# SyncE's transfers in the order of the program, and the last exchange's first round behind the residual's load

## The chip, the core and the metric

The kernel runs on one core of a Trainium2 chip. TensorE multiplies, VectorE, ScalarE and GpSimd work on the results, and SyncE only issues transfers (DMAs). Each engine runs its own list of instructions strictly in the order in which they stand there, and waits for the others by semaphores. The metric is the device time of one execution in microseconds.

## The reference

Attention with a conditioning vector, over 8 batches of 512 rows, 512 features and 16 heads of 32, and the input is added at the end:

```python
Q = _split_heads(x @ Wq.T + bq)
K = _split_heads(x @ Wk.T + bk)
V = _split_heads(x @ Wv.T + bv)
tQ = _split_heads(tokens @ Wq.T + bq)
tK = _split_heads(tokens @ Wk.T + bk)
cQ = Q + tQ
cK = K + tK
scores = jnp.einsum('bhqd,bhkd->bhqk', cQ, cK) / jnp.sqrt(jnp.float32(HEAD_DIM))
attn = jax.nn.softmax(scores, axis=-1)
out = jnp.einsum('bhqk,bhkd->bhqd', attn, V)
...
x = x + attention
```

## The kernel before

**Tiles and stages.** Work is cut into 32 tiles, numbered 0 to 31: tile t is batch t // 4 and a group of four heads. A loop calls `thirds(t)` for the tiles 1 to 28; one call is a stage. What stands ahead of the loop (loads, tile 0, the beginning of tile 1) and behind it (tiles 29 to 31) is written out by hand. A stage finishes tile t-1 (`weighted`: the product of its softmax weights with V, L839, then its sums, its output), computes row maxima and part of the weights of tile t+1, the rest of the weights of tile t, and three pieces of the projections of a later batch. The stage's parts i = 0, 1, 2 are the three thirds. A stage begins, on TensorE, with the L839 matmuls of `weighted`.

**Two halves of the weights.** For the first 256 query rows of a tile the weights that were made for the row maxima are kept (`kept`, in `store`); for the other 256 they are computed again in the transposed form that the product needs. `weighted` takes the fresh half first and the kept half second. The kept half has to be transposed. VectorE turns its 32x32 blocks in four pieces (`turn_kept`, L659: two pieces in the first third of the stage before its own, one at the end of each other third), and the blocks are then exchanged between groups of 32 partitions by transfers.

**The exchange.** `swap_kept(t, move)` has three rounds of six transfers (L681): move 0 puts a block aside, move 1 copies its partner into its place, move 2 brings the one put aside to the partner's place. Each transfer waits for the landing of the one ahead of it in its chain of three. In an ordinary tile SyncE issues two of move 0 and all of move 1 (eight), GpSimd four of move 0 and all of move 2; in every fourth tile SyncE issues all of move 0 too (twelve). For the last kept tile, 29, SyncE issues move 0 and half of each of the others. Moves 0 and 1 of tile t+1 stand at the end of stage t, move 2 in the middle third of stage t+1, ahead of `split_max` (GpSimd, L714 to L717) and `turn_max` of the following tile.

**SyncE's other transfers.** In each stage: `send` writes the output of tile t-1 (L916, four transfers, after GpSimd's last addition, L913); `load_blocks` loads four pieces of x for a later batch (L172, until x is used up in stage 22), which VectorE turns (L371); `turn_max` transposes the maxima (maxT, L726, after GpSimd's L717), which TensorE needs at L771; `load_residual` loads x again for the last addition (xr, L190, four pieces), to which GpSimd adds the bias (`bias_residual`, L203). Tile 30's residual goes into `store`. A transfer also waits for the one eight places ahead of it on its queue.

**What sets the order.** The order of TensorE, ScalarE, VectorE and GpSimd is that of the program, because the call `manual_schedule` names these four. SyncE isn't named: a scheduler of the framework places its transfers by its own estimate of when each becomes ready, so that a load whose buffer is free may be put ahead of, or among, transfers that the program writes earlier.

Of the kernel before, what the change touches and what calls it, by code (L numbers as in the profile page):

```python
# [17 lines left out]
def kernel(  # L18
# [52 lines left out]
    KEPT = range(1, T - 2)  # L71
# [59 lines left out]
    def begin(*ws):  # L131
        for w in ws:
            rows = order[w : w + 4]
            pairs = [(j, j + 1) for j in rows if j + 1 in rows]
            last = max(
                pairs, key=lambda p: rows.index(p[0]) + rows.index(p[1]), default=sorted(rows[2:])
            )
            order[w : w + 4] = [j for j in rows if j not in last] + list(last)
        row_of[0] = list(order)

    def released(*roles):
        order[:] = [row_of[0][i] for i in roles]
# [19 lines left out]
    def spread(a, d):  # L162

        return a.rearrange("(f j) d -> j f d", j=BL)[:, :, d : d + BL]
# [12 lines left out]
    def turned_by_vector(t):  # L177

        return t < T - 1

    def load_residual(t):

        b, g = divmod(t, G)
        if turned_by_vector(t):
            if t == T - 2:
                xr[t] = late[0][:, 2, :].rearrange("p (f e) -> p f e", e=BL)
            else:
                xr[t] = op.tile([P, NB, BL], F32, tag="xr", name=f"xr_{t}")
            for h in range(HG):
                nc.sync.dma_start(  # L190
                    xr[t][h * BL : (h + 1) * BL], spread(x[b], g * P + h * BL)
                )
        else:

            xr[t] = xT[b][:, g, :]
# [31 lines left out]
    def load_w(n, w, queue, cs=range(NC)):  # L227
        wv = w.rearrange("(c p) d -> p c d", p=P)
        for c in cs:
# [7 lines left out]
                mybir.EngineType.Activation,  # L237
                mybir.EngineType.DVE,
                mybir.EngineType.Pool,
            }  # L240
        )
    )
# [353 lines left out]
    def row_max(t, qc, hold=False, w=HG, scores=True):  # L596

        if t >= T:
            return
        open_max(t)  # L600
        for j in range(HG if scores else 0):
            row_scores(t, qc, j, banks(w + j))
        if row_of[0] or t < T - 2 or t * NS + qc == T * NS - 1:
            for j in range(2) if scores else (1, 0):
                one_max(t, qc, j, banks(w + j))
        else:
            row_max_of(t, qc, 0, banks(w, 2))
        last, both = [banks(w + 2), banks(w + 3)], banks(w + 2, 2)
        apart = row_of[0] and row_of[0][w + 3] - row_of[0][w + 2] > 1

        def held():
            if apart or hold and t < T - 2:
                for j in range(2):
                    one_max(t, qc, 2 + j, last[j])
            else:
                row_max_of(t, qc, 1, both)

        if hold:
            return held
        held()  # L620
        return nothing
# [4 lines left out]
    def row_max_aside(t, qc):  # L626

        open_max(t)
        for j in range(HG):
            row_scores(t, qc, j, banks(j))  # L630
        nc.scalar.copy(spare, banks(0).rearrange("p (c f) -> p c f", f=P))  # L631
        for j in (1, 2, 3):
            one_max(t, qc, j, banks(j))

    def max_aside(t, qc):
        nc.vector.tensor_reduce(nmax[t][:, qc, 0:1, 0], spare, AX.XY, ALU.max, negate=True)
# [27 lines left out]
    def swap_kept(t, move, some=range(6)):  # L664

        later = 6 if t % 4 == 1 else 2

        def part(a, g):
            return kept[t][a * BL : (a + 1) * BL, g].rearrange("p c h s -> p (c h s)")

        for n in some:
            a, g = APART[n]
            at = (n + 2) % HG * BL
            aside = (store[:, 6:8] if t == KEPT[-1] else between)[at : at + BL, n // HG]
            aside = aside.rearrange("p i s -> p (i s)")
            to, of = [(aside, part(a, g)), (part(a, g), part(g, a)), (part(g, a), aside)][move]
            if t < KEPT[-1]:
                here = move == 2 or move == 0 and n >= later
            else:
                here = move > 0 and n >= 3  # L680
            (nc.gpsimd if here else nc.sync).dma_start(to, of)  # L681

    def denominators(t, qc, w=HG, js=range(HG)):

        if t >= T - 2:
            return
        keep = t in KEPT and qc < KQ
        if keep and t not in kept:
            kept[t] = room(t)
        for j in js:  # L690
            of = to = banks((w or 0) + j)
            if w is None and j == 0:
                of = to = spare
            if keep:
                to = kept[t][:, :, qc, j, :].rearrange("p g (c e) -> p g c e", e=BL)
                if w is None and j == 0:
                    of = spare.rearrange("p c (g e) -> p g c e", e=BL)
                else:
                    of = of.rearrange("p (c g e) -> p g c e", g=HG, e=BL)
            nc.scalar.activation(  # L700
                to,
                of,
                AF.Exp,
                bias=nmax[t][:, qc, j, :],
                accum_out=sums[t][:, qc, j, :],
            )
# [437 lines left out]
    def turn_more(t, i, after):  # L1144

        for _ in range((TURNED if t + 1 < KEPT[-1] else TURNED_LAST).get((i, after), 0)):
            if t + 1 in KEPT:
                n = turned[t + 1] = turned.get(t + 1, -1) + 1
                turn_kept(t + 1, n)
        even = t % 2 == 0  # L1150
        if (i, after) == ((2, 1) if even else (0, 2)) or (t, i, after) == (2, 0, 2):
            turn_x(next_x[0])
            next_x[0] += 1

    def thirds(t, made):

        b, r = divmod(t, G)
        of = (t - 1) // G + 1
        begin(0, HG)
        turn_more(t, 0, 0)  # L1160
        row_max_aside(t + 1, 1)
        max_aside(t + 1, 1)
        row_max(t + 1, 2, False, HG)
        turn_more(t, 0, 1)
        denominators(t + 1, 1, None, (1, 2, 3, 0))
        denominators(t + 1, 2, HG)
        weighted(t - 1, banks(0), banks(1), nothing)
        turn_more(t, 0, 2)
        load_blocks(1)
        one_item(of, *next(made), (2, 3), ignore, nothing)  # L1170
        released(0, 1, 4, 5, 7, 6, 2, 3)
        for i in (1, 2):
            begin(HG)
            rows = (t + 1, 3) if i == 1 else (t + 2, 0)
            if i == 1:
                joined(t, i - 1, rows)
                turn_more(t, i, 0)
                row_max(*rows, False, HG, False)
            else:
                exponentials_of_rest(t, i - 1)  # L1180
                turn_more(t, i, 0)
                row_max(*rows, False, HG)
            turn_more(t, i, 1)
            if i == 1:
                first = range(6 if t + 1 < KEPT[-1] else 3)
                swap_kept(t, 2, first)
                split_max(t + 1)
                turn_max(t + 1)
                swap_kept(t, 2, range(len(first), 6))
            dens = lambda js=range(HG): denominators(*rows, HG, js)  # L1190
            n, u, kind = next(made)
            if kind == "first":
                products(of, n, u, kind, False, dens, nothing, None)
                turn_more(t, i, 2)
            elif n == "v":
                small = nothing
                if t + 1 not in KEPT:
                    small = lambda: transpose_max(t + 1, banks(2), nc.scalar.copy)
                other_shared(of, n, u, dens, (0, 3), small, lambda: turn_more(t, i, 2))
                released(1, 2, 4, 5, 6, 7, 0, 3)  # L1200
            else:
                products(of, n, u, kind, False, dens, nothing, False)
                turn_more(t, i, 2)
            if i == 1:
                aparts[t] = masked(t)
            if (t + 1, i) == (KEPT[-1], 1):
                swap_kept(t + 1, 0)
            if i == 2:
                if r == 0:
                    combine_x(b + 1, 1, nc.gpsimd)  # L1210
                load_residual(t + 1)
            else:
                if t > 1:
                    bias_residual(t)
                if r == 0:
                    combine_x(b + 1, 0, nc.gpsimd)
            if i == 2 and t + 1 < KEPT[-1]:
                for move in range(2):
                    swap_kept(t + 1, move)
# [105 lines left out]
    t = T - 3  # L1325
# [46 lines left out]
    t = T - 2  # L1372
# [25 lines left out]
    t = T - 1  # L1398
# [101 lines left out]
```

## Time and profile before

| what | value |
|---|---|
| median of 3 runs | 649.41 us (649.39 to 649.48) |
| the profiled execution | 650.74 us |
| its span, first to last instruction | 648.9 us |
| granted TensorE clock | 1.000 |
| TensorE matmuls busy | 642.6 us (99%) |
| TensorE weight loads busy | 358.5 us (55%) |
| VectorE, ScalarE, GpSimd busy | 600.7 us (93%), 533.6 us (82%), 409.6 us (63%) |
| SyncE's queue of transfers, share of the 16 DMA engines | 53.3% |
| GpSimd's queue of transfers | 19.2% |

The times are from the start of the profiled span. A row of the view in order of time reads: start, duration, engine, line, operation, what is written from what is read, how many; in square brackets stands the idle time of the engine ahead of it and what ended it. Consecutive equal instructions are one row. SPq is SyncE issuing transfers: its duration is the time of issue (with the waits between the transfers of one row), not of the transfer, which lands later. In the section of the page on transfers the last number is the median time from issue to landing. "issue" as a releaser means that the view shows no other engine that ended the wait.

### The profile page before, as it was taken

To read this page: it belongs to the slowest core of one execution; us is meant where nothing else is said; L and a number is where in the kernel's file an instruction comes from. 1 tells how busy PE (TensorE), PEld (TensorE's weight loads), DVE (VectorE), ACT (ScalarE), POOL (GpSimd) and SP (SyncE) were. 2 spreads that over 40 slices of the span, in tenths; PEclk is the share of its full clock that TensorE was granted. 3 is DMA by queue.
4 is the path that set the end of the run, shared out by engine and by line. 5 is a ranking of instruction groups with operands and counts; after the bars stand their busy time and mean duration, and the time that the engine had idled before them with its cause. 6 is when DMAs were issued, how large, how long until landed. Compare 5 with 4: busy or idle time off the path is not lost. (4 is left out here: it accounts for less than half of the span.)

```text
span 648.9 us, 24878 instructions
## 1 busy us (share of the span) xinstructions
PE 642.6 (99%) x9856; PEld 358.5 (55%) x9856; DVE 600.7 (93%) x845; ACT 533.6 (82%) x1364; POOL 409.6 (63%) x651
## 2 busy tenths in 40 slices
PE   9999999999999999999999999999999999999997
PEld 8445555556555555555555555555655555555541
DVE  3799999999999999999999999999999999999887
ACT  2479888889888889888888988898988888888564
POOL 3642555767666785668566585766767677675650
PEclk9999999999999999999999999999999999999999
DMA  7634588788779788878788887897877777777821
GB/s 187 106 48 68 121 183 175 158 180 178 155 172 181 156 190 181 190 155 172 173 184 172 171 170 152 177 198 158 180 152 180 176 162 153 165 177 161 201 37 33
DMA packets 248456, 102.01 MB, mean 157 GB/s; under 512 B 229962, under 2 KB 230474, under 8 KB 248340
## 3 DMA queue, kind: packets, MB, share of 16 engines
q1 hardware_dynamic: 234196, 65.54, 53.3%
q0 software_dynamic: 12384, 33.83, 19.2%
q8 instruction: 78, 1.28, 0.8%
q10 hardware_dynamic: 1760, 1.05, 0.6%
q14 instruction: 38, 0.31, 0.2%
HBM read 19.75 MB, written 8.39 MB: 43 GB/s over the span
## 5 line engine op out<-in xcount | busy, mean ns | idle before, releaser
L592 DVE TENSOR_REDUCE nmax<-psum 128x1 f32<-128x512 f32 x279 | 177.8, 676 | 9.9 <-PE psum L640 5.1
L681 POOL DMA_DIRECT2D store<-store x258 | 128.9, 502 | 77.3 <-DMA store<-store 51.9
L700 ACT ACTIVATE psum<-psum,nmax 128x512 f32<-128x512 f32 x248 | 165.1, 678 | 3.6 <-DVE nmax L592 3.0
L640 PE MATMUL psum<-kT,qT 32*128 32x512 f32 x1024 | 161.8, 612 | 0.0
L700 ACT ACTIVATE store<-psum,nmax 128x512 f32<-128x512 f32 x204 | 139.5, 700 | 24.7 <-DVE nmax L592 24.5
L798 ACT ACTIVATE store<-psum 128x512 f32<-128x512 f32 x232 | 119.8, 603 | 33.4 <-PE psum L784 33.4
L659 DVE STREAM_TRANSPOSE store<-store 128x1024 f32<-128x1024 f32 x116 | 138.9, 1217 | 0.0
L649 DVE TENSOR_REDUCE nmax<-psum 128x2 f32<-128x1024 f32 x98 | 118.9, 1213 | 0.0
L839 PE MATMUL psum<-store,v 128*32 128x256 f32 x1856 | 107.1, 381 | 0.6 <-issue 0.6
L839 PEld LDWEIGHTS psum<-store,v 128*32 128x32 f32 x1856 | 57.2, 110 | 57.9 <-ACT wT_q L631 21.2
L784 PE MATMUL psum<-qT,kT 32*128 32x256 f32 x928 | 83.8, 373 | 0.0
L640 PEld LDWEIGHTS psum<-kT,qT 32*128 32x128 f32 x1024 | 61.3, 183 | 35.5 <-issue 17.8
L912 POOL TENSOR_TENSOR res<-res,recs 128x512 f32<-128x512 f32 x30 | 31.4, 1045 | 75.4 <-DVE res L911 75.4
L784 PEld LDWEIGHTS psum<-qT,kT 32*128 32x128 f32 x928 | 60.8, 184 | 5.7 <-issue 0.3
L700 ACT ACTIVATION_READ_ACCUMULATOR psum<-psum,nmax 128x1 f32 x248 | 55.1, 222 | 0.0
L461 PE MATMUL psum<-wc_v,xc 128*32 128x256 f32 x768 | 47.7, 379 | 0.0
L203 POOL TENSOR_TENSOR xr<-xr,bvs 128x512 f32<-128x512 f32 x30 | 38.3, 1276 | 11.1 <-DMA x<-in_x_dram 11.1
L461 PE MATMUL psum<-xc,wc_q 128*32 128x256 f32 x720 | 44.8, 379 | 0.0
L461 PE MATMUL psum<-xc,wc_k 128*32 128x256 f32 x720 | 44.5, 379 | 0.0
L700 ACT ACTIVATION_READ_ACCUMULATOR store<-psum,nmax 128x1 f32 x204 | 44.4, 218 | 0.0
L913 POOL TENSOR_TENSOR res<-res,xr 128x512 f32<-128x512 f32 x30 | 38.3, 1276 | 2.4
L461 PE MATMUL psum<-xT,wT_k 128*32 128x256 f32 x480 | 34.5, 382 | 0.0
(191 smaller groups left out, 975.4 us busy)
## 6 DMA issues: line engine op xcount, KB each, us to landing
store<-store SPq DMA_DIRECT2D x264, 128.0 KB, 2.9
store<-store POOLq DMA_DIRECT2D x258, 128.0 KB, 3.8
out_dram<-res SPq DMA_DIRECT2D x122, 64.0 KB, 3.7
xr<-in_x_dram SPq DMA_DIRECT2D x120, 64.0 KB, 3.4
x<-in_x_dram SPq DMA_DIRECT2D x112, 64.0 KB, 3.5
w_q<-in_L_cond_Wq_dram SPq DMA_DIRECT2D x4, 256.0 KB, 4.5
w_v<-in_L_cond_Wv_dram SPq DMA_DIRECT2D x16, 64.0 KB, 2.5
w_k<-in_L_cond_Wk_dram SPq DMA_DIRECT2D x16, 48.0 KB, 2.8
```

What stands on the lines that cost most here:

```text
L203: nc.gpsimd.tensor_tensor(xr[t], xr[t], bias, ALU.add)
L461: nc.tensor.matmul(pt[r], still[:, r], moving, start=(kc == kcs[0]), stop=(kc == kcs[-1]))
L592: nc.vector.tensor_reduce(nmax[t][:, qc, j : j + 1, 0], pt, AX.X, ALU.max, negate=True)
L640: nc.tensor.matmul(pt, qkT["q", t][r, qc * P : (qc + 1) * P], qkT["k", t][r, :], start=True, stop=True,)
L649: nc.vector.tensor_reduce(nmax[t][:, qc, pr * 2 : pr * 2 + 2, 0], pt, AX.X, ALU.max, negate=True)
L659: nc.vector.transpose(e, e)
L681: (nc.gpsimd if here else nc.sync).dma_start(to, of)
L700: nc.scalar.activation(to, of, AF.Exp, bias=nmax[t][:, qc, j, :], accum_out=sums[t][:, qc, j, :],)
L784: nc.tensor.matmul(banks(j)[:, i * HS : (i + 1) * HS], qkT["k", t][r, kc * P : (kc + 1) * P], qkT["q", t][r, KQ * P :], start=False, stop= ...
L798: nc.scalar.activation(e[:, j], banks(j), AF.Exp)
L839: nc.tensor.matmul(pt[j * HD : (j + 1) * HD, half * HS : (half + 1) * HS], vs[b % 2][:, kc, (g * HG + j) * HD : (g * HG + j + 1) * HD], e, ...
L913: nc.gpsimd.tensor_tensor(y, y, xr.pop(t), ALU.add)
```

## The change

SyncE is named in the call as well, so that its transfers stand in the order in which the program's text issues them. And in stage 28 the residual of tile 29 is loaded in the middle third, ahead of move 0 of tile 29's exchange, and no longer in the last third.

```diff
                 mybir.EngineType.DVE,
                 mybir.EngineType.Pool,
+                mybir.EngineType.SP,
             }
...
             if (t + 1, i) == (KEPT[-1], 1):
+                load_residual(t + 1)
                 swap_kept(t + 1, 0)
             if i == 2:
                 if r == 0:
                     combine_x(b + 1, 1, nc.gpsimd)
-                load_residual(t + 1)
+                if t + 1 < KEPT[-1]:
+                    load_residual(t + 1)
```

The lists of TensorE, VectorE, ScalarE and GpSimd are the same, row by row; the lines of the new file are one to three higher. SyncE's list has the same transfers in another order. In the rows that follow, the number behind xr, maxT and res is the tile; behind x it counts blocks of x (four to a batch); store is the exchange. A row gives the line, the operation, written from read, the shape and how many.

SyncE in stages 21 and 22, before: the exchange of tiles 21 (twelve) and 22 (two and six).

```order
L726 DMA_TRANSPOSE maxT_21_6002<-split_145 128x4x128
L190 DMA xr_21_6114<-in_x_dram 32x16x32
L172 DMA x_30_6204<-in_x_dram 32x16x32 x3
L681 DMA store_77<-store_77 32x1024 x12
L916 DMA out_0_dram<-res_20_6193 32x16x32 x4
L172 DMA x_30_6204<-in_x_dram 32x16x32
L726 DMA_TRANSPOSE maxT_22_6277<-split_145 128x4x128
L190 DMA xr_22_6380<-in_x_dram 32x16x32 x4
L172 DMA x_31_6469<-in_x_dram 32x16x32 x2
L681 DMA store_77<-store_77 32x1024 x2
L172 DMA x_31_6469<-in_x_dram 32x16x32
L681 DMA store_77<-store_77 32x1024 x6
```

The same place in the changed kernel:

```order
L727 DMA_TRANSPOSE maxT_21_6002<-split_145 128x4x128
L190 DMA xr_21_6114<-in_x_dram 32x16x32 x4
L682 DMA store_77<-store_77 32x1024 x12
L917 DMA out_0_dram<-res_20_6193 32x16x32 x4
L172 DMA x_30_6204<-in_x_dram 32x16x32 x4
L727 DMA_TRANSPOSE maxT_22_6277<-split_145 128x4x128
L190 DMA xr_22_6380<-in_x_dram 32x16x32 x4
L682 DMA store_77<-store_77 32x1024 x8
```

The loads of x no longer stand ahead of or within an exchange; all four stand behind the output and ahead of maxT. The load of xr stands whole between maxT and the exchange; before, some of it stood ahead of maxT in three of four stages.

SyncE at the start, before (tiles 0 and 1, and the blocks of batch 1 and 2, which wait for VectorE from x_6 on):

```order
L172 DMA x_5_246<-in_x_dram 32x16x32 x4
L190 DMA xr_0_553<-in_x_dram 32x16x32 x4
L172 DMA x_6_492<-in_x_dram 32x16x32 x4
L190 DMA xr_1_620<-in_x_dram 32x16x32
L172 DMA x_7_548<-in_x_dram 32x16x32 x4
L190 DMA xr_1_620<-in_x_dram 32x16x32 x3
L172 DMA x_8_615<-in_x_dram 32x16x32 x4
```

And now:

```order
L172 DMA x_5_246<-in_x_dram 32x16x32 x4
L172 DMA x_6_492<-in_x_dram 32x16x32 x4
L172 DMA x_7_548<-in_x_dram 32x16x32 x4
L190 DMA xr_0_553<-in_x_dram 32x16x32 x4
L172 DMA x_8_615<-in_x_dram 32x16x32 x4
L190 DMA xr_1_620<-in_x_dram 32x16x32 x4
```

Each residual moved behind the blocks that the program writes ahead of it: two for tile 0, one more for tile 1.

SyncE at the last exchange (tile 29), before; the rows of store from in_x are the residual of tile 30:

```order
L916 DMA out_0_dram<-res_27_8024 32x16x32 x4
L190 DMA xr_29_8205<-in_x_dram 32x16x32 x2
L726 DMA_TRANSPOSE maxT_29_8093<-split_145 128x4x128
L190 DMA xr_29_8205<-in_x_dram 32x16x32 x2
L190 DMA store_77<-in_x_dram 32x16x32
L681 DMA store_77<-store_77 32x1024 x12
L190 DMA store_77<-in_x_dram 32x16x32 x3
```

And now:

```order
L917 DMA out_0_dram<-res_27_8024 32x16x32 x4
L727 DMA_TRANSPOSE maxT_29_8093<-split_145 128x4x128
L190 DMA xr_29_8137<-in_x_dram 32x16x32 x4
L682 DMA store_77<-store_77 32x1024 x12
L190 DMA store_77<-in_x_dram 32x16x32 x4
```

Two loads moved from ahead of maxT to between maxT and the exchange, and one load of tile 30's residual from ahead of the exchange to behind it.

## The prediction

> **What bounds the kernel now.** I read the page first, then TensorE's rows in order of time, then the rows of GpSimd and SyncE in the stages where TensorE's pace breaks. Two lines of the page: the span, and TensorE's busy time.
>
> ```profile
> span 648.9 us, 24878 instructions
> PE 642.6 (99%) x9856; PEld 358.5 (55%) x9856; DVE 600.7 (93%) x845; ACT 533.6 (82%) x1364; POOL 409.6 (63%) x651
> ```
>
> TensorE has work on it for all but 6.3 us, but matmuls overlap, so that a busy row may hide a wait. I check the pace. Every stage (one head group of one batch) begins with L839, the product of the weights with V. Here it is at the start of stages 14, 18, 22 and 26:
>
> ```profile
> 317.70 3.66 PE L839 MATMUL psum<-store,v 128*32 128x256 f32 x64
> ...
> 394.28 3.66 PE L839 MATMUL psum<-store,v 128*32 128x256 f32 x64
> ...
> 471.00 3.66 PE L839 MATMUL psum<-store,v 128*32 128x256 f32 x64
> ...
> 548.43 3.66 PE L839 MATMUL psum<-store,v 128*32 128x256 f32 x64
> ```
>
> Four stages take 76.58 us (394.28 - 317.70), then 76.72, then 77.43. If 76.58 is TensorE's own pace, 0.14 and 0.85 us were lost in these two blocks of four. They are found in L839 itself: the 64 matmuls that take 3.66 us above take longer at the start of stages 19 and 23.
>
> ```profile
> 413.44 3.79 PE L839 MATMUL psum<-store,v 128*32 128x256 f32 x64
> ...
> 490.15 1.93 PE L839 MATMUL psum<-store,v 128*32 128x256 f32 x32
> 492.73 1.50 PE L839 MATMUL psum<-store,v 128*32 128x256 f32 x24 [0.64 <-issue]
> ```
>
> At 413.44 it is 3.79 - 3.66 = 0.13 us. At 490.15 the first half (the fresh weights) runs at pace, and the second, which reads the kept weights after their exchange between partitions, starts 0.64 us after the end of the first. The profile writes "issue"; the row that fits is the exchange's last transfer, issued by GpSimd:
>
> ```profile
> 488.41 0.49 POOL L681 DMA_DIRECT2D store<-store x1 [0.68 <-DMA store<-store]
> ...
> store<-store POOLq DMA_DIRECT2D x258, 128.0 KB, 3.8
> ```
>
> 488.41 plus the median 3.8 us to landing is 492.2; TensorE goes on 0.5 us later. So the kernel is bound by TensorE, and transfers have cost it some 0.98 us in all. This is nearly all that an order of transfers can give back; the rest of the question is what it can take.
>
> **The change part by part.** Nothing is added or removed: 699 instructions of SyncE before and after, and the rows of the other engines keep their order. Only SyncE's queue changes, so every cost is a cost of lateness.
>
> *The steady stages.* SyncE's rows of the stage that led to the stall, the exchange of tile 22:
>
> ```profile
> 470.87 1.21 SPq L726 DMA_TRANSPOSE maxT<-split  x1
> 472.13 3.69 SPq L190 DMA_DIRECT2D xr<-in_x_dram  x4
> 475.92 1.30 SPq L172 DMA_DIRECT2D x<-in_x_dram  x2
> 477.39 1.16 SPq L681 DMA_DIRECT2D store<-store  x2
> 478.60 0.58 SPq L172 DMA_DIRECT2D x<-in_x_dram  x1
> 479.73 4.92 SPq L681 DMA_DIRECT2D store<-store  x6
> 484.74 3.33 SPq L916 DMA_DIRECT2D out_dram<-res  x4
> 488.12 0.61 SPq L172 DMA_DIRECT2D x<-in_x_dram  x1
> 488.77 0.87 SPq L190 DMA_DIRECT2D xr<-in_x_dram  x1
> 490.16 1.65 SPq L726 DMA_TRANSPOSE maxT<-split  x1
> ```
>
> In the order of the program the three loads of x at 475.92 and 478.60 leave this stretch. The exchange then starts when the residual's load is issued, at 475.9 instead of 477.39: 1.5 us earlier. The second row of loads (0.58) had filled a wait of 1.1 us for the first round's landing (477.92 or so to 479.73), so nothing is saved there. The end moves from 484.65 to about 483.1, GpSimd's last transfer from 488.41 to 486.9, and its landing from 492.2 to 490.7, 1.3 us before TensorE asks at 492.0 (490.15 + half of 3.66). The 0.85 us goes, and the 0.13 with less to spare. What is late next: maxT of the next tile now stands behind four stores of out and four loads of x: 483.1 + 3.3 + 2.5 = 488.9, against 490.16 before, and xr, now wholly behind it, is issued by 488.9 + 1.2 + 3.7 = 493.8. The next exchange thus starts where it did (493.66), and no later.
>
> The loads of x that move back are issued by 488.9 and land, with the same 3.8 us, at 492.7. Their reader is VectorE's turn in the next stage:
>
> ```profile
> 497.95 0.67 DVE L371 STREAM_TRANSPOSE xT<-x 128x512 f32<-128x512 f32 x1
> ```
>
> 5.2 us are to spare, and I price this at nothing. If that cover went, VectorE (93% busy) would wait, and TensorE after it.
>
> *Stages without loads of x* (24 to 28). There SyncE waits for VectorE's fourth turn:
>
> ```profile
> 510.21 8.69 SPq L681 DMA_DIRECT2D store<-store  x8
> 529.36 9.05 SPq L681 DMA_DIRECT2D store<-store  x12
> 548.53 7.65 SPq L681 DMA_DIRECT2D store<-store  x8
> 567.68 9.00 SPq L681 DMA_DIRECT2D store<-store  x8
> ...
> 519.48 2.96 POOL L681 DMA_DIRECT2D store<-store  x6
> ...
> 529.26 3.66 PE L839 MATMUL psum<-store,v 128*32 128x256 f32 x64
> ```
>
> All four loads of xr come behind maxT, at most 4 x 0.9 = 3.7 us (the row at 472.13) in front of the exchange. For tile 24, GpSimd's last issue at about 521.9 lands at 525.7; TensorE asks at 529.26 + 1.83 = 531.1. The margin is 5.4 us and takes the worst case; it costs nothing.
>
> *The start.* xr of tile 0 now stands behind two loads that wait for VectorE, and xr of tile 1 behind a third:
>
> ```profile
> 49.20 2.65 SPq L190 DMA_DIRECT2D xr<-in_x_dram  x3
> 52.09 9.03 SPq L172 DMA_DIRECT2D x<-in_x_dram  x8
> ...
> 54.15 1.28 POOL L203 TENSOR_TENSOR xr<-xr,bvs 128x512 f32<-128x512 f32 x1 [11.06 <-DMA x<-in_x_dram]
> 61.28 0.25 POOL L714 CAST split<-nmax 128x16 bf16<-128x16 f32 x1 [5.85 <-DVE nmax L592]
> ```
>
> The bias at 54.15 came 2.3 us after the last issue (51.85). Now the first four loads of x at 52.09 end at about 54.1, xr of tile 1 follows until 56.3, the bias can start at 58.6 and end at 59.9; GpSimd is wanted for the next maxima only at 61.28. Cost nothing, with 1.4 us to spare.
>
> *The last exchange* (tile 29), the second edit:
>
> ```profile
> 598.85 1.22 SPq L726 DMA_TRANSPOSE maxT<-split  x1
> 600.11 1.11 SPq L190 DMA_DIRECT2D xr<-in_x_dram  x2
> 601.33 0.43 SPq L190 DMA_DIRECT2D store<-in_x_dram  x1
> 601.87 10.74 SPq L681 DMA_DIRECT2D store<-store  x12
> ...
> 613.78 0.49 POOL L681 DMA_DIRECT2D store<-store  x1 [0.61 <-DMA store<-store]
> 619.06 1.93 PE L839 MATMUL psum<-store,v 128*32 128x256 f32 x32
> ```
>
> Behind maxT there are now four loads of xr (2.2 us) and none into store: the exchange starts at 602.4, 0.5 us later. Its end was 613.78 + 3.8 = 617.6, plus the 0.5 us that TensorE needed above 618.1; it becomes 618.6, before 619.06. Cost 0, at worst some 1.5 us.
>
> **The sum.** 0.98 us less in the profiled execution, which took 650.74 us (span 648.9 and 1.84 around it): 649.76. The median of the three runs is 649.41, 1.33 us below that one, so the stalls may belong to profiling; the gain lies between 0 and 0.98. The runs agree to 0.09 us, so the stall is in all of them or in none; I take it as in all: 649.41 - 0.98 = **648.4 us**. A measurement of this kernel can tell about 0.2%, 1.3 us, from no change.
>
> **The rivals.**
> *The stalls were the profiler's alone, or another stall takes their place* (the change doesn't do what it might): 649.4. For it: the 1.33 us. Against: the waits follow from an order that is the same in every run.
>
> *SyncE becomes the bound.* With the new order nothing fills its waits. From the rows, a stage with loads of x needs 1.21 + 3.69 + 3.33 + 2.49 (x: 1.30 + 0.58 + 0.61) = 10.72 us beside the exchange; with 7.65 to 9.00 for it, 18.4 to 19.7 us, and 19.8 with twelve transfers (9.05), against 19.15 per stage. At the upper end the queue falls back 0.57 us in each of 17 stages and 0.6 in each of five, 12.7 us; less the 5.4 us of margin TensorE would lose 7; midway, 3.5 us, the time is near 652. It decides from 19.4 us a stage on (5.4 / 22 above 19.15). Against it: the new out and x stand apart from the exchange, and the wait between two rounds shrinks when the exchange starts late (479.73 ended a wait of 1.1 us). The Trainium skill's page Perfetto Trace Analysis, section What "DMA-bound" means, names an issuing sequencer whose track is solid with transfers as a bound of its own; the rows above, solid but for some 2 us, agree that SyncE is close, and by that rule this rival would be the forecast.
>
> *The last exchange stalls TensorE*: 0.5 to 1.5 us of the gain given back, 649.0 to 649.9.
>
> *TensorE has room under its 99%*, and earlier transfers speed up more than the two stalls. Weight loads waited for the exchange at another place too:
>
> ```profile
> PEld L771 <- DMA store<-store: 2.5, 6, 0.4
> ```
>
> If those 2.5 us counted as well: 648.4 - 2.5 = 645.9; half of it, 647.1. Against: the pace of 76.58 us is the same wherever L839 isn't late. The same page, section Identifying the Most-Contended Engine, says that matmul occupancy doesn't show how near the limit TensorE is, and weight-load occupancy does: by that rule the 55% leave room; the constant pace speaks against it here.
>
> **How the numbers follow.** Forecast 0.52 (648.0 to 649.0), nothing gained 0.20, SyncE bound 0.12, last exchange 0.08, room on TensorE 0.08. Faster by over 0.2% (below 648.1): the last, and 0.06 of the forecast, 0.14. Slower (above 650.7): SyncE's case and 0.02 of the last exchange, 0.14. The rest 0.72. The range takes the forecast, the two cases near 649.4 and the near parts of the others: 647.6 to 650.8.
>
> **What would show it.** Right: four stages take 76.6 us throughout, L839 is 3.66 us at every start, SyncE's x rows lie between out and maxT, and the exchange starts 0 to 3 us into a stage. Wrong: L839 split by "issue" in more stages than before, growing from stage to stage (SyncE bound); a gap before the product at 619 (last exchange); GpSimd's bias beyond 61 us (start).

## The result and the profile after

The changed kernel takes 653.98 us (median of 22 runs, 650.53 to 661.77), the kernel before 650.85 us beside it (22 runs, 649.15 to 654.02). The ratio is **1.0049 [1.0029, 1.0068]**: the change made the kernel slower by half a per cent. The forecast was 648.4 us. Both kernels vary more from run to run than the three runs shown before (649.39 to 649.48).

The profiled execution of the changed kernel took 658.46 us, 7.72 us more than the one of before, so it lies on the slow side of its 22 runs. It is read here for where the time goes, not for how much. Its lines are one to three higher: L839 is L840, L771 is L772, L681 is L682, L726 is L727. Two lines of its page:

```profile
span 656.7 us, 24840 instructions
PE 645.6 (98%) x9856; PEld 361.1 (55%) x9856; DVE 601.3 (92%) x845; ACT 534.6 (81%) x1364; POOL 410.3 (62%) x651
```

TensorE's rows in order of time: the product with V (L840) that begins each stage, and the matmuls that read maxT (L772) where TensorE stood idle ahead of them.

```profile
106.46 3.66 PE L840 MATMUL psum<-store,v 128*32 128x256 f32 x64
...
278.72 3.66 PE L840 MATMUL psum<-store,v 128*32 128x256 f32 x64
...
286.92 0.40 PE L772 MATMUL psum<-maxT,onesb 3*128 3x512 bf16 x4 [1.89 <-DMA maxT<-split]
...
348.38 0.40 PE L772 MATMUL psum<-maxT,onesb 3*128 3x512 bf16 x4 [1.20 <-DMA maxT<-split]
...
360.81 1.93 PE L840 MATMUL psum<-store,v 128*32 128x256 f32 x32
363.89 1.93 PE L840 MATMUL psum<-store,v 128*32 128x256 f32 x32 [1.15 <-DMA x<-in_x_dram]
...
498.08 1.93 PE L840 MATMUL psum<-store,v 128*32 128x256 f32 x32
```

From 106.46 to 278.72 there are nine stages of 19.14 us: TensorE's own pace (76.58 / 4), nothing lost. From 278.72 to 498.08 there are eleven of 19.94 us, and 8.8 us are lost (219.36 - 11 x 19.145). The view of waits has 5.5 us of it as idle time of TensorE (3.5 + 1.7 + 0.3); the rest lies inside rows that count as busy (645.6 us against 642.6). The waits stand at two places: ahead of the kept half of the product with V, as before the change (the row names a load of x, which the product doesn't read; what it reads is the exchange), and, new, ahead of the matmuls that read maxT.

SyncE's rows in the same execution: maxT of tile 3, the round from the exchange of tile 12 to that of tile 13, and maxT of tile 23.

```profile
103.79 1.21 SPq L727 DMA_TRANSPOSE maxT<-split  x1
...
264.75 8.62 SPq L682 DMA_DIRECT2D store<-store  x8
273.46 3.01 SPq L917 DMA_DIRECT2D out_dram<-res  x4
276.51 3.52 SPq L172 DMA_DIRECT2D x<-in_x_dram  x4
280.14 2.21 SPq L727 DMA_TRANSPOSE maxT<-split  x1
282.40 4.07 SPq L190 DMA_DIRECT2D xr<-in_x_dram  x4
286.64 8.18 SPq L682 DMA_DIRECT2D store<-store  x8
...
499.65 1.21 SPq L727 DMA_TRANSPOSE maxT<-split  x1
```

The maxT issued at 103.79 is 2.67 us ahead of its stage (106.46), the one at 280.14 is 1.42 us behind (278.72): nine stages, 4.09 us, on average 0.45 us later with each. It doesn't come evenly: to tile 6, issued at 160.98, SyncE keeps pace, and the six rounds from there to 280.14 take 19.86 us each. SyncE's round is longer than a stage, and up to stage 12 nobody sees it, since the margin is being used up. From 280.14 to 499.65 SyncE takes 19.96 us a stage and TensorE 19.94: the two now go at one pace, and the experiments below show that it is SyncE's. (In two of these rounds SyncE itself waited for GpSimd ahead of maxT, 1.58 us at 360.98 and 0.57 us at 400.65; GpSimd has the exchange's last round ahead of maxT's input, so a late exchange comes back that way too.) Between 264.75 and 286.64 one row follows the other within 0.2 us, and that one round takes 21.9 us, one of the longest; inside its row of eight stores the view has waits of 2.6 us.

What the queue waits for is in the view of waits (us in total, times, longest), of before and then of the changed kernel:

```profile
SPq L681 <- DMA store<-store: 44.4, 39, 3.3
```

```profile
SPq L682 <- DMA store<-store: 59.8, 38, 4.1
```

This is the wait for the landing of the first round, ahead of the second. It grew by 15.4 us; in the window from 120 to 430 us, about sixteen stages with loads of x, the same view has 24.0 and 28.1 us, so that only 4.1 us of the growth lie there; 7.6 us stand behind 499 us, where x is used up (9.0 and 16.6 up to 600 us). The wait is thus not all of what made a round longer.

The kernel before was near this limit as well. Its maxT of tile 4 was issued 2.16 us ahead of its stage (124.05 against 126.21), that of tile 19 0.46 us behind, and that of tile 23 with its stage (490.16 against 490.15, both in the prediction). These are the two stages, 19 and 23, whose L839 was late.

```profile
413.90 1.25 SPq L726 DMA_TRANSPOSE maxT<-split  x1
```

### The profile page after: what moved, and what is told of

Same layout as the page of the kernel before. It is cut to its first block, busy times and chain, and to the rows that moved or that the text cites. A ratio compares the mean times of both kernels' runs of the same rounds, so it can differ in the third digit from the quotient of the medians.

```text
span 656.7 us, 24840 instructions
## 1 busy us (share of the span) xinstructions
PE 645.6 (98%) x9856; PEld 361.1 (55%) x9856; DVE 601.3 (92%) x845; ACT 534.6 (81%) x1364; POOL 410.3 (62%) x651
## 5 line engine op out<-in xcount | busy, mean ns | idle before, releaser
L682 POOL DMA_DIRECT2D store<-store x258 | 129.1, 504 | 86.7 <-DMA store<-store 59.8
L641 PE MATMUL psum<-kT,qT 32*128 32x512 f32 x1024 | 164.3, 613 | 0.0
L840 PE MATMUL psum<-store,v 128*32 128x256 f32 x1856 | 108.0, 381 | 2.1 <-DMA x<-in_x_dram 1.7
L840 PEld LDWEIGHTS psum<-store,v 128*32 128x32 f32 x1856 | 57.6, 110 | 59.8 <-ACT wT_q L632 21.2
L462 PE MATMUL psum<-xT,wT_q 128*32 128x256 f32 x480 | 34.7, 380 | 0.0
```

Source lines behind the costliest of these rows:

```text
L462: nc.tensor.matmul(pt[r], still[:, r], moving, start=(kc == kcs[0]), stop=(kc == kcs[-1]))
L641: nc.tensor.matmul(pt, qkT["q", t][r, qc * P : (qc + 1) * P], qkT["k", t][r, :], start=True, stop=True,)
L840: nc.tensor.matmul(pt[j * HD : (j + 1) * HD, half * HS : (half + 1) * HS], vs[b % 2][:, kc, (g * HG + j) * HD : (g * HG + j + 1) * HD], e, ...
```

## The experiments

**Queue theory**: the scheduler had put loads of x into the wait between the first two rounds of an exchange (the trace of before shows it in every fourth stage, as at 478.60). In the order of the program nothing stands there, so that SyncE's round gets longer than a stage, and its lateness adds up until maxT and the exchange come too late. **Landing theory**: the round fits; maxT lands late because the eight transfers of out and x stand right ahead of it. **End theory**: the second edit, at the last exchange, is what costs. A fourth, the **collision theory**, came from the trace later on. Each experiment was timed against the kernel before on the same chip, with medians of 650.3 to 651.3 us. All edits are to the changed kernel unless something else is said.

**The order alone.** The second edit is undone:

```diff
             if (t + 1, i) == (KEPT[-1], 1):
-                load_residual(t + 1)
                 swap_kept(t + 1, 0)
...
-                if t + 1 < KEPT[-1]:
-                    load_residual(t + 1)
+                load_residual(t + 1)
```

> SyncE's order of the program alone; tile 29's residual is still loaded behind the first round of its exchange. Queue theory (SyncE goes round exchange, out, x, maxT, xr, exchange, one behind the other, and this round with its waits takes more than a stage's 19.15 us, so that maxT and the exchange come later from stage to stage): as the changed kernel, ratio to the kernel before 1.003 to 1.007, maxT issued up to 1.5 us behind a stage's start around stages 10 to 23. Landing theory (the round fits, but maxT lands late, up to 7 us, because eight transfers of out and x stand right ahead of it in the DMA engines): the same 1.003 to 1.007. End theory (the second edit, the residual ahead of the last exchange, is what costs): 1.000, and no gap on TensorE ahead of L771.

Measured: 657.80 us, ratio 1.0077 [1.0049, 1.0106]. The order of SyncE's queue costs what was seen, without the second edit. The end theory falls. Whether the second edit helps can't be read from this pair: the interval overlaps that of the whole change.

**The second edit alone.** Before's kernel, SyncE with the scheduler, the residual ahead of the last exchange's first round:

```diff
             if (t + 1, i) == (KEPT[-1], 1):
+                load_residual(t + 1)
                 swap_kept(t + 1, 0)
...
-                load_residual(t + 1)
+                if t + 1 < KEPT[-1]:
+                    load_residual(t + 1)
```

> The second edit alone: SyncE stays with the scheduler's order, and only the residual of tile 29 is put ahead of the first round of its exchange. Queue theory and landing theory alike: the steady stages are those of before, so 651.3 us, ratio 1.000 (0.998 to 1.002), TensorE's stages of 19.10 to 19.17 us except for the one or two late ones of before. The end theory (this edit is what costs): 1.003 to 1.005, with a gap of over 1 us ahead of the last product with V, near 619 us.

Measured: 649.92 us, 0.9995 [0.9977, 1.0014]. No difference that can be told: in the scheduler's order the second edit costs less than 0.2%.

**Loads of x behind the exchange**, ahead of the output, no longer right ahead of maxT:

```diff
-        load_blocks(1)
+        if t < 3:
+            load_blocks(1)
...
                 for move in range(2):
                     swap_kept(t + 1, move)
+                if t > 1:
+                    load_blocks(1)
```

> The changed kernel with the loads of x behind the exchange and ahead of out, so that only out stands right ahead of maxT; as many transfers in a round as before. Queue theory: nothing gained, ratio 1.003 to 1.007, maxT still waits for SyncE and not for GpSimd in most stages from 9 to 23. Landing theory: maxT has half as many transfers ahead of it, lands within 4 us, no gap on TensorE ahead of maxT's first matmul: 1.000 or less.

Measured: 651.64 us, 1.0007 [0.9992, 1.0021]. The loss is nearly gone: the queue theory, which expected all of it, missed, and this run alone would speak for the landing theory. But SyncE's rows drift here too, from an earlier start: maxT of tile 3 is issued 4.82 us ahead of its stage (102.11 against 106.93), that of tile 19 1.26 us into it (414.87 against 413.61), 0.38 us later with each stage. TensorE pays there:

```profile
413.61 1.93 PE L840 MATMUL psum<-store,v 128*32 128x256 f32 x32
415.86 1.93 PE L840 MATMUL psum<-store,v 128*32 128x256 f32 x32 [0.31 <-DMA x<-in_x_dram]
```

So this order is at its limit as well, and x runs out (stage 22) before the loss can grow. That reading is argued from one trace, of the shortest of this kernel's executions (650.35 us), while that of the changed kernel is of one of its longest. From tile 3 to tile 23 its round is 19.45 us long, that of the changed kernel 19.79; why it is shorter, with the wait just as empty, stays open. The two runs that follow decide between the theories.

**Loads of x between the two rounds:**

```diff
-                for move in range(2):
-                    swap_kept(t + 1, move)
+                swap_kept(t + 1, 0)
+                if t > 1:
+                    load_blocks(1)
+                swap_kept(t + 1, 1)
```

(and `if t < 3` as above.)

> The changed kernel with the loads of x between the first and the second round of the exchange, where SyncE waits for the first round's landing. Queue theory: the loads fill a wait of 1 to 2.4 us, the round gets that much shorter, maxT waits for GpSimd in most stages and comes ahead of a stage's start: ratio 0.998 to 1.001; the exchange ends about as late as in the changed kernel or 1 us later. Landing theory: x no longer stands ahead of maxT: also 0.998 to 1.001, but with the round as long as before, so that maxT still waits for SyncE.

Measured: 651.11 us, 0.9998 [0.9983, 1.0013]. SyncE's waits, two lines of that view:

```profile
SPq L727 <- POOL apart L865: 30.8, 19, 2.5
SPq L682 <- DMA store<-store: 27.4, 21, 2.9
```

The wait for landings halves (27.4 against 59.8), and maxT is now held up by GpSimd, which makes its input (the row names the operation on GpSimd right behind it): SyncE is early and waits for others, as a queue does that bounds nothing.

**xr between the two rounds, x left where the change put it**, right ahead of maxT. This separates the two theories:

```diff
-                if t + 1 < KEPT[-1]:
-                    load_residual(t + 1)
...
-                for move in range(2):
-                    swap_kept(t + 1, move)
+                swap_kept(t + 1, 0)
+                load_residual(t + 1)
+                swap_kept(t + 1, 1)
```

> The changed kernel with the four loads of the residual xr moved from ahead of the exchange to between its first and second round, where SyncE waits for landings. The loads of x stay where the change put them, right ahead of maxT. Queue theory (the round got too long because nothing fills that wait): SyncE's round is 1.5 to 2.5 us shorter, maxT is issued 2 us or more ahead of its stage and waits for GpSimd, not for SyncE; 651.2 us, ratio 1.000. Landing theory (x right ahead of maxT): landings of 6 to 7 us stay whatever the round's length, 653 to 654 us, 1.003 to 1.005. Collision theory: as the queue theory, since maxT is no longer late enough to meet GpSimd's first round.

Measured: 650.45 us, 0.9993 [0.9981, 1.0006]. The landing theory falls: out and x stand ahead of maxT, eight transfers, and nothing is lost. SyncE's rows over one round of this kernel, to be laid beside the round of the changed one:

```profile
275.71 1.21 SPq L727 DMA_TRANSPOSE maxT<-split  x1
278.79 1.17 SPq L682 DMA_DIRECT2D store<-store  x2
280.01 3.79 SPq L190 DMA_DIRECT2D xr<-in_x_dram  x4
283.90 5.07 SPq L682 DMA_DIRECT2D store<-store  x6
289.07 3.51 SPq L917 DMA_DIRECT2D out_dram<-res  x4
292.63 4.39 SPq L172 DMA_DIRECT2D x<-in_x_dram  x4
```

The same eight stores take 1.17 + 5.07 = 6.24 us where their rows, with the waits inside them, took 8.62 and 8.18; the residual's 3.79 us run while the first round lands. Behind maxT (276.92) the queue stands idle for 1.87 us. The view of waits says for whom:

```profile
SPq L682 <- DVE store L660: 32.7, 19, 5.0
SPq L682 <- DMA store<-store: 1.9, 4, 0.9
```

The exchange now waits for VectorE's fourth turn (32.7 us), that is, for its own data, and hardly at all for landings (1.9 against 59.8). Filling that wait is enough to undo the loss, and x and the residual's loads serve alike. maxT was still often held up by SyncE here, where the queue theory expected GpSimd and 2 us or more ahead of the stage, but it was never issued less than 0.70 us ahead of it.

**x alternating**: each second load of x between the rounds, the others as the change puts them. It tests whether lateness is carried from stage to stage:

```diff
-        load_blocks(1)
+        if t < 3 or t % 2:
+            load_blocks(1)
...
+                swap_kept(t + 1, 0)
+                if t > 1 and t % 2:
+                    load_blocks(1)
+                swap_kept(t + 1, 1)
```

> The changed kernel with every second load of x between the two rounds of the exchange, the others where the change puts them, behind the output and ahead of maxT. Queue theory (SyncE's lateness is carried from stage to stage, about 0.4 us more with each stage in the changed order, and given back in a stage whose wait is filled): maxT's issue swings from stage to stage without growing, stays ahead of 0.5 us into its stage, and nothing is lost: 650.5 us, ratio 1.000. Rival (each stage with the changed order costs its share by itself): half the loss stays, 652 us, 1.0025.

Measured: 649.64 us, 0.9993 [0.9980, 1.0005]. Nothing of the loss stays, though half of the stages have the changed order. SyncE's rows of maxT, which bound two rounds, the first without and the second with x in the wait:

```profile
255.33 1.86 SPq L727 DMA_TRANSPOSE maxT<-split  x1
...
275.66 1.21 SPq L727 DMA_TRANSPOSE maxT<-split  x1
...
294.20 2.38 SPq L727 DMA_TRANSPOSE maxT<-split  x1
```

The first round is 20.33 us long (275.66 - 255.33), the second 18.54 (294.20 - 275.66), and there SyncE even waits 0.84 us for GpSimd ahead of maxT (its output ends at 293.36): a stage's excess of 1.2 us is given back by the next. The rival, by which half of the loss had to stay (1.0025), lies outside the interval. A queue that is late costs nothing by itself; one that gets later with every stage does.

**The collision theory.** In the changed kernel's four stages with the longest way from maxT's issue to its landing, GpSimd's four transfers of the next exchange's first round start in the same microsecond. GpSimd's rows at two of them:

```profile
279.87 2.00 POOL L682 DMA_DIRECT2D store<-store  x4
...
340.77 2.00 POOL L682 DMA_DIRECT2D store<-store  x4
```

maxT was issued at 280.14 and at 341.29, and TensorE's waits for it ended at 286.92 and 348.38, some 7 us later. To keep them apart, eight small copies on GpSimd go ahead of its four transfers:

```diff
+                if (t + 1) % 4 != 1:
+                    for _ in range(8):
+                        nc.gpsimd.tensor_copy(idle, kept[t + 1][:, 0, 1, 2, :16])
                 for move in range(2):
                     swap_kept(t + 1, move)
```

> The changed kernel, with eight small copies on GpSimd (about 2.5 us, in time in which it waits) ahead of its four transfers of an exchange's first round, so that these no longer start together with a late maxT. SyncE's list is that of the changed kernel, loads of x still right ahead of maxT. Collision theory (maxT lands late because GpSimd's first round, four transfers of 128 KB, starts at the same moment): maxT lands within 4.5 us in every stage instead of 6 to 7 in four of them, and the time falls to that of the loads behind the exchange, 651.6 us, ratio 1.001. Landing theory (the eight transfers of out and x ahead of maxT): landings of 6 to 7 us stay, 654 us, 1.005. Queue theory in its plain form (only the length of SyncE's round counts): the round is as long or longer, maxT is issued over 1 us into its stage from stage 12 on, 654 us or more, 1.005 to 1.008.

Measured: 670.58 us, 1.0281 [1.0242, 1.0319]. No theory had the time. The landings went as the collision theory has them: a line of the view of maxT's row, for the changed kernel and then for this one:

```profile
DMA to landing us min/median/max: 2.5/3.7/7.1
```

```profile
DMA to landing us min/median/max: 2.5/3.3/4.6
```

But SyncE's second round waits for GpSimd's share of the first. Pushed back by 2 us, it makes SyncE's round longer still where nobody waits for SyncE yet (20.38 us on average from maxT of tile 3, at 105.73, to that of tile 8, at 207.63; 19.56 in the changed kernel), and TensorE waits ahead of the kept half instead. GpSimd's copies and its share of the first round in this kernel, in order of time, and then the largest row of TensorE's waits (the load that it names is again not what L840 reads):

```profile
206.14 2.02 POOL L1223 CAST idle<-store 128x16 bf16<-128x16 f32 x8
208.20 2.00 POOL L682 DMA_DIRECT2D store<-store  x4
```

```profile
PE psum L840 <- DMA x<-in_x_dram: 7.3, 4, 4.2
```

So shorter landings don't help where the round gets longer. How much a collision costs by itself stays open: this run changes both at once.

**The output by GpSimd.** The four transfers of out leave SyncE's round:

```diff
-            nc.sync.dma_start(spread(out[b], g * P + h * BL), y[h * BL : (h + 1) * BL])
+            (nc.gpsimd if 0 < t < T - 4 else nc.sync).dma_start(
+                spread(out[b], g * P + h * BL), y[h * BL : (h + 1) * BL]
+            )
```

> The changed kernel with the outputs of tiles 1 to 27 issued by GpSimd, right behind its last addition: four issues (2.2 to 4 us) leave SyncE's round, GpSimd gets four of about 0.5 us. The number of transfers is the same, and x stands right ahead of maxT as in the changed kernel. Queue theory: maxT waits for GpSimd in most stages, no gap ahead of maxT's first matmul: ratio 0.998 to 1.001. Landing theory: maxT still lands up to 6 or 7 us late behind x: 1.002 to 1.006.

Measured: 679.13 us, 1.0439 [1.0406, 1.0472]. SyncE is relieved: maxT is issued ahead of every stage, and no wait for it is left. The bound moved to GpSimd. GpSimd, VectorE and TensorE around one such place, in one view:

```profile
316.77 2.63 POOL L917 DMA_DIRECT2D out_dram<-res  x4 [0.29 <-POOL res L914]
319.42 0.75 POOL L539 TENSOR_TENSOR qT<-qT 128x256 f32<-128x256 f32 x1
...
321.00 0.42 DVE L555 TENSOR_TENSOR qT<-psum,qT 128x256 f32<-128x256 f32 x1 [1.81 <-POOL qT L540]
...
321.59 2.68 PE L641 MATMUL psum<-kT,qT 32*128 32x512 f32 x8
```

The 2.63 us of issue stand on GpSimd ahead of additions for which VectorE waits, and eight matmuls that take 1.14 us elsewhere take 2.68. Every second stage becomes 20.82 us instead of 19.15, two of them longer still (22.58 and 22.20), which over 13 of them is 25 us. The Trainium skill's page Perfetto Trace Analysis, section DMA Optimizations, says that balancing transfers across the engines that can issue them may help when issuing is the bottleneck. Here it took the bottleneck away and made the kernel 4.4% slower, because the other engine had only 0.29 us of idle time ahead of the four transfers and VectorE waited for what came behind them.

**x between the rounds, xr behind the exchange**, so that nothing stands between maxT and the exchange:

```diff
-                if t + 1 < KEPT[-1]:
-                    load_residual(t + 1)
...
+                swap_kept(t + 1, 0)
+                if t > 1:
+                    load_blocks(1)
+                swap_kept(t + 1, 1)
+                load_residual(t + 1)
```

> Loads of x between the two rounds of the exchange and the residual's loads behind it, so that nothing stands between maxT and the exchange. Queue theory: SyncE's round has the most slack of all orders, the exchange starts 2 us earlier than with x alone moved, and the last waits of TensorE for the exchange (about 1 us in the profile of before) go: 650.3 us, ratio 0.998 to 0.9995. Rival: the residual's loads, now ahead of the output and maxT, make maxT late by their 2 to 3 us: maxT waits for SyncE again and 651.5 to 652.5 us, 1.0005 to 1.002.

Measured: 651.71 us, 1.0021 [1.0007, 1.0036]. The rival's time, but not at its place: the steady stages run at pace, and TensorE waits once, at the last exchange.

```profile
620.10 1.93 PE L840 MATMUL psum<-store,v 128*32 128x256 f32 x32 [1.98 <-DMA store<-store]
```

xr of tile 28, now ahead of the last output and maxT, starts tile 29's exchange later, at 604.25, against 602.19 with xr between the rounds, where TensorE waited 0.49 us at this place.

**xr between the rounds, at tile 29 too**, to take the last 0.49 us:

```diff
             if (t + 1, i) == (KEPT[-1], 1):
-                load_residual(t + 1)
                 swap_kept(t + 1, 0)
...
+                if t + 1 == KEPT[-1]:
+                    load_residual(t + 1)
```

(the other tiles as in the run with xr between the rounds.)

> The residual's loads between the first and second round of every exchange, that of tile 29 too (which the changed kernel puts ahead of that exchange's first round). Queue and end theory together (a load in the wait between two rounds costs nothing, one ahead of an exchange delays it by its 2.2 us): the steady stages keep their 19.10 to 19.17 us, the last exchange starts right behind maxT, 2.2 us earlier, and the 0.49 us by which TensorE waited for it near 618 us goes: 650.0 us, ratio 0.997 to 0.999. Rival (the last exchange is bound by its chain of landings, not by its start): it ends where it did, the 0.5 us stays, 650.5 us, 0.999 to 1.000.

Measured: 651.72 us, 1.0013 [1.0000, 1.0027]. Both expectations missed. GpSimd's rows:

```profile
609.81 1.27 POOL L203 TENSOR_TENSOR xr<-xr,bvs 128x512 f32<-128x512 f32 x1 [3.89 <-DMA xr<-in_x_dram]
611.02 1.52 POOL L682 DMA_DIRECT2D store<-store  x3
```

The exchange starts 1.4 us earlier (600.76 against 602.19), but GpSimd's list has the bias of this very residual ahead of its half of the second round. It waits 3.89 us for the late xr, its three transfers follow at 611.02, and TensorE waits 1.95 us for the exchange. This is what the change's second edit guards against. The wait is read from one trace each (1.95 us here, 0.49 with the residual ahead of the last exchange); the times' intervals overlap.

## Why the prediction was wrong, point by point

- **What bounds the kernel.** Right for before: TensorE's pace of 19.145 us a stage, with small losses to late transfers. That an order can give back no more than about 1 us fits all runs as well. With x alternating, twenty stages take 382.90 us, 19.145 each, no loss left, and the time is still not to be told from that of before.

```profile
125.47 3.66 PE L840 MATMUL psum<-store,v 128*32 128x256 f32 x64
...
508.37 3.66 PE L840 MATMUL psum<-store,v 128*32 128x256 f32 x64
```

- **The steady stages: here it failed**, at the sentence "The next exchange thus starts where it did (493.66), and no later." It put together one stage's round, 7.2 us of exchange, 3.3 of out, 2.5 of x, 1.2 of maxT and 3.7 of xr, 17.9 us in all, out of rows of the old order, and took it for every stage. Two of its terms were too small. The stage that it read is one of the few where a load of x stood between the two rounds, so that the wait left there was short; the rows of stages without x, 7.65 to 9.05 us, which the text itself used for its rival, are those of an exchange with an empty wait. The means of one round, from maxT of tile 4 to that of tile 23 (added up from SyncE's rows, waits inside a row included):

| us per round | before | changed kernel | xr between the rounds |
|---|---|---|---|
| exchange | 7.45 | 8.18 | 6.60 |
| x | 2.84 | 3.37 | 3.17 |
| out | 3.18 | 3.42 | 3.28 |
| xr | 3.06 | 2.88 | 3.33 |
| maxT | 1.31 | 1.41 | 1.55 |
| idle between rows | 1.43 | 0.56 | 1.26 |
| the round | 19.27 | 19.82 | 19.19 |

  The exchange measured 8.18 us for 7.2, the loads of x 3.37 for 2.5; xr was overrated by 0.8. That x and out took longer to issue than before is measured, the reason stays open. And one stage's sum was taken for all: an excess of half a microsecond is small in a stage, and 4.09 us after nine.
- **maxT** was computed at 488.9 for 490.16 in that stage and dropped. Its lateness was the first thing that TensorE met (286.92). The margin of 5.4 us that the rival was reckoned with is that of an exchange in a stage without x; in the stage with x the same text had 1.3 us, and its rows had maxT issued at the stage's very start.
- **SyncE becomes the bound**, the rival with 12 chances in 100, is what happened, nearly as priced: a round of 18.4 to 19.8 us, deciding from 19.4, near 652 us. Measured: 19.79 us in the profiled execution from tile 3 to tile 23, 653.98 us. The mechanism was right; the nearness of the time is partly luck, as the price was the middle of 0 to 7 us and the single runs lie anywhere from 650.53 to 661.77 us. The Trainium skill's page Perfetto Trace Analysis, section What "DMA-bound" means, whose rule of a sequencer solid with transfers stood beside this rival, would have made it the forecast, and it came true. But "solid" is not what the traces show: SyncE's rows fill 299 of the 310 us from 120 to 430 us in the changed kernel, 288 in the one before and 302 with x behind the exchange, which lost nearly nothing; and in the changed kernel 44.1 of these 310 us are waits by the view of waits, most of them inside rows. The length of the round tells more.
- **The chance against it** rested in part on the wait between two rounds shrinking when the exchange starts late. It grew, from 44.4 to 59.8 us in all, also in the window of the steady stages (24.0 to 28.1).
- **x later for VectorE**: cost nothing, as said. No wait of VectorE for x is in the view.
- **Stages without x**: right. From stage 24 on maxT waits for GpSimd again and TensorE is at pace.
- **The start**: right. The bias of tile 1 was expected to end by 59.9 and to leave GpSimd free in time. Two of its rows:

```profile
57.98 1.28 POOL L203 TENSOR_TENSOR xr<-xr,bvs 128x512 f32<-128x512 f32 x1 [2.69 <-DMA xr<-in_x_dram]
60.61 0.26 POOL L715 CAST split<-nmax 128x16 bf16<-128x16 f32 x1 [1.35 <-DVE nmax L593]
```

- **The last exchange**: no gap in the changed kernel, whose TensorE is late by then. Where the steady stages are in time there mostly is one, which the rival had at 0.5 to 1.5 us: 0.25 us with x alternating, 0.93 with x between the rounds, 1.98 and 1.95 in the last two runs, none with x behind the exchange (in the first two the row names ScalarE as what ended it). This is the row of the kernel with xr between the rounds, 0.49 us.

```profile
618.17 1.93 PE L840 MATMUL psum<-store,v 128*32 128x256 f32 x32 [0.49 <-DMA store<-store]
```

- **Room on TensorE under its 99%**: none. No order went below 19.145 us a stage.
- **The absolute time**: the three runs near 649.41 were taken as the kernel's spread. Beside the changed kernel, before had a median of 650.85 over 22 runs and a spread of 4.9 us, so "in all of them or in none" didn't hold.

What would have beaten both kernels by more than a measurement can tell was not found: the best orders, xr between the rounds or x alternating, have 0.9993 with intervals that take in 1.

## What to carry to other kernels

Where an engine issues transfers strictly in order, add up its whole round in the new order, waits included, against the length of a stage: here an excess of half a microsecond added up until every margin was gone, and then the queue set the pace. Put transfers that nobody waits for into the waits that a chain of transfers forces on its queue, whichever transfers these are, and look at what stands behind each wait on every engine that shares the chain. Before moving transfers to another engine, look for idle time there at the very place where they would stand.

## What was unexpected of the hardware

- Issue times on SyncE were not constant: four loads of x took 2.69 us in one round of the changed kernel (298.83) and 4.39 us in one of the kernel with xr between the rounds (292.63), with nothing between them that the profile shows as a wait.

```profile
298.83 2.69 SPq L172 DMA_DIRECT2D x<-in_x_dram  x4
```

- The way of the small transposing transfer from issue to landing spread from 2.5 to 7.1 us. The trace tells the landing of 16 of the 29. All four above 5.9 us had GpSimd's four transfers of 128 KB starting within 0.9 us of it; other such meetings took 3.4 to 4.5 us. That they cause it was not isolated.
